# ScalarE takes a third batch of the neighbour rows in the second graph-attention layer

## The chip, the cores and the metric

The kernel runs on one core of a Trainium2 chip. TensorE (PE) multiplies, VectorE (DVE) works element by element and reduces, ScalarE (ACT) applies functions with a scale, GpSimd (POOL) issues the indirect DMAs and SyncE (SP) the plain ones. The metric is the device time of one execution in microseconds. Times are medians of several executions; a difference under 0.3% (10.3 us) is about what a measurement of this kernel cannot tell from no change.

## The reference

There are four layers on x (8 batches, 2048 nodes, 128 features) and one adjacency matrix with 0.8% ones. Layers 0 and 1 are transformer layers with masked attention. Layers 2 and 3 are graph-attention (GAT) layers:

```python
h = x @ W                                   # x: (8, 2048, 128)
e = (h @ a_src)[:, :, None] + (h @ a_dst)[:, None, :]
e = where(e >= 0, e, 0.2 * e);  e = where(adj == 0, -inf, e)
out = einsum('bij,bjd->bid', softmax(e), h)
y = out + x
x = layernorm(y) * ln_gamma + ln_beta
```

## The kernel before, in words

The nodes are sorted by their number of neighbours and cut into 16 tiles of 128 nodes, one node to a partition. `CAPS` (line 38) gives how many neighbour columns each tile has, from 30 down to 11, 277 in all. For every layer a table in device memory has one row per node. In layers 2 and 3 a row has 1040 floats: the projected features of the 8 batches (8 x 128) and two exponentials of the source score for each batch. The neighbours of a tile are fetched column by column: `gather` (line 319, the DMA on line 320) is one indirect DMA by GpSimd that brings the row of the k-th neighbour of each of 128 nodes.

In the GAT layers up to four columns form a chunk. A chunk lands in one of six buffers (`KVB`, line 31), and `gat_chunk` (line 736) is a generator with four steps:

1. DVE finishes the two exponentials (L753), takes their maximum, which is the softmax weight, for all batches into PSUM (`pair`, L754), and once more into a small SBUF tile `ws` for the batches that ACT will scale (L759).
2. DVE multiplies the feature rows of the first `nv` batches with their weights in one instruction (L765). ACT multiplies those of the last `SCALED` batches, one instruction for each column and batch (L770), reading its weight from `ws`.
3. DVE adds the second half of the columns to the first half, all batches (L774).
4. PE adds the remaining columns into the accumulator in PSUM with an identity matrix (L780).

The order is written out by hand: each engine executes its instructions in the order in which the Python code records them. The loop in `layers` (line 1169) records for chunk c steps 1 and 2 and then steps 3 and 4 of the chunk before it, so L774 of chunk c-1 stands behind L765 of chunk c on DVE. Between the steps `slot` (line 1120) advances the tails of finished tiles by one step each and calls `fetch` (line 1096), which records the gathers of chunks up to four ahead. A buffer's new gathers therefore stand in GpSimd's queue behind whatever was recorded earlier, and wait for the PE instructions that last read the buffer.

When the last chunk of a tile is through, `outputs` (L657) divides by the sum of weights and `gat_tail` (line 786) follows: PE adds the residual (L801, L805, L810), ACT squares with an accumulated sum (L817), GpSimd takes the power -1/2 (`rs`, L844), ACT scales by it (L825). In layer 2 the result is then transposed and projected (L329, L832, L535, L549 to L555) and `put_rows` (L502) scatters it into the next layer's table. In layer 3 the layer norm's gain and offset follow on DVE (L858, L860) and GpSimd scatters the tile to the output (L862). In layer 3 the tile `rows`, of which there is one, holds the squares and then the result, so L817 of the next tile waits until L862 has landed.

Layer 3 starts before layer 2 is through: the first two tiles have their neighbour lists sorted by when the neighbour's row is written, and `ORDER` (line 43) puts seven chunks of them first; `fetch` (L1106) holds their gathers until enough tiles of the table are written. While that lasts, `hurry` (line 1115) advances the tails more often.

Of the kernel before, what the change touches and what calls it, by code (L numbers as in the profile page):

```python
# [8 lines left out]
F32 = mybir.dt.float32  # L9
# [8 lines left out]
P = 128  # L18
# [10 lines left out]
NB = 8  # L29
CHUNK = 4 * NB * (D + 2)  # L30
KVB = 6
SCALED = 2

# [47 lines left out]
def sparse_path(ctx: ExitStack, tc: tile.TileContext, ins: dict, out: bass.AP, flag: bass.AP):  # L83
# [10 lines left out]
    nc = tc.nc  # L94
    const = ctx.enter_context(tc.tile_pool(name="const", bufs=1))
    work = ctx.enter_context(tc.tile_pool(name="work", bufs=2))
    small = ctx.enter_context(tc.tile_pool(name="small", bufs=2))
# [5 lines left out]
    def misc():  # L103
        return pm.tile([P, 512], F32, tag="m", name="m")
# [36 lines left out]
    bufs = [const.tile([P, CHUNK], F32, name=f"kv{i}") for i in range(KVB)]  # L141
# [300 lines left out]
    def folded_sums(w, box):  # L442

        columns = w.shape[-1]
        ps = misc()[:, :columns]
        for i in range(FOLD):
            nc.tensor.matmul(ps, merge, w[:, i, :], start=i == 0, stop=i == FOLD - 1)
        box["folded"] = small.tile([P, columns], F32, tag="folded", name="folded", bufs=1)
        nc.scalar.copy(box["folded"], ps)
# [286 lines left out]
    def gat_chunk(l, c):  # L736
        box, t, k, ns = c["box"], c["t"], c["k"], c["ns"]
        mine = own[:, t, :]
        if c["folded"]:
            pf = misc()[:, :NB]  # L740
            nc.tensor.matmul(pf, spread, mine, start=True, stop=True)
            mine = small.tile([P, NB], F32, tag="mine", name="mine", bufs=1)
            nc.scalar.copy(mine, pf)
            yield
        if k == 0:
            box["acc"] = pacc.tile([P, NB // 4, 512], F32, tag="acc", name="acc")
            at, n = (0 if t % 2 == 0 else 512 - NB * CAPS[t]), CAPS[t]
            box["w"] = pair[:, at : at + NB * n].rearrange("p (s b) -> p s b", b=NB)
        acc, w = box["acc"], box["w"]
        hs = c["buf"]  # L750
        wc = w[:, k : k + ns, :]
        wa, wb = hs[:, :, NB * D : NB * (D + 1)], hs[:, :, NB * (D + 1) :]
        nc.vector.tensor_mul(wb, wb, mine[:, None, :].to_broadcast([P, ns, NB]))  # L753
        nc.vector.tensor_max(wc, wa, wb)  # L754
        if c["folded"]:
            box["wf"] = small.tile([P, FOLD, NB], F32, tag="wf", name="wf", bufs=1)
            nc.vector.tensor_max(box["wf"], wa, wb)
        ws = small.tile([P, 4, SCALED], F32, tag="ws", name="ws", bufs=3)
        nc.vector.tensor_max(  # L759
            ws[:, :ns, :], wa[:, :, NB - SCALED :], wb[:, :, NB - SCALED :]  # L760
        )
        yield
        hv = hs[:, :, : NB * D].rearrange("p s (b c) -> p s b c", b=NB)
        nv = NB - SCALED
        nc.vector.tensor_mul(  # L765
            hv[:, :, :nv, :], hv[:, :, :nv, :], wc[:, :, :nv, None].to_broadcast([P, ns, nv, D])
        )
        for i in range(ns):
            for b in range(nv, NB):
                nc.scalar.mul(hv[:, i, b, :], hv[:, i, b, :], ws[:, i, b - nv : b - nv + 1])  # L770
        yield
        left = -(-ns // 2)
        if ns > 1:
            nc.vector.tensor_add(hv[:, : ns - left], hv[:, : ns - left], hv[:, left:ns])  # L774
        yield
        if c["folded"]:
            folded_sums(box["wf"], box)
        for i in range(left):
            for j in range(NB // 4):
                nc.tensor.matmul(  # L780
                    acc[:, j, :], merge if c["folded"] else ident, hv[:, i, 4 * j : 4 * j + 4, :],
                    start=k + i == 0, stop=c["last"] and i == left - 1,
                )
        yield
# [296 lines left out]
    for l in range(4):  # L1081
        per = 2 if l < 2 else 4
        for t, k, ns, folded in pieces(l, per):
            c = dict(l=l, t=t, k=k, ns=ns, folded=folded, box=blocks[l][t])
            c["last"] = not folded and k + ns == (CAPS[t] if t > 0 else BASE)
            c["run"] = (attention_chunk if l < 2 else gat_chunk)(l, c)
            every.append(c)
# [660 lines left out]
```

## Time and profile before

| | |
|---|---|
| device time, median of 3 runs | 3423.61 us (3417.87 to 3426.96) |
| the profiled execution | 3428.05 us, span 3426.3 us |
| layer 2 alone, about | 2220 to 2840 us of the span |
| layer 3, its first chunks among the last tails of layer 2 | from about 2813 us of the span |
| layer 3 alone | about 2884 us to the end |
| busy in 2884 to 3365 us (481 us) | DVE 405.50, POOL 374.36, PE 338.82, ACT 209.82 us; DMA engines 88% |

In a list of instructions a line has the start and the duration in us, the engine, the source line, the operation, the tiles written and read, and a count of equal instructions that followed one another; in brackets stands how long the engine had been idle before it and what released it. In the table of groups, a line has the count, the busy time, the mean duration of one instruction in ns (a third number is idle time before the group) and the releasers.

### The profile page before, as it was taken

To read this page: it belongs to the slowest core of one execution; us is meant where nothing else is said; L and a number is where in the kernel's file an instruction comes from. 1 tells how busy PE (TensorE), PEld (TensorE's weight loads), DVE (VectorE), ACT (ScalarE), POOL (GpSimd) and SP (SyncE) were. 2 spreads that over 40 slices of the span, in tenths; PEclk is the share of its full clock that TensorE was granted. 3 is DMA by queue.
4 is the path that set the end of the run, shared out by engine and by line. 5 is a ranking of instruction groups with operands and counts; after the bars stand their busy time and mean duration, and the time that the engine had idled before them with its cause. 6 is when DMAs were issued, how large, how long until landed. Compare 5 with 4: busy or idle time off the path is not lost.

```text
span 3426.3 us, 34767 instructions
## 1 busy us (share of the span) xinstructions
PE 2761.3 (81%) x10618; PEld 1595.4 (47%) x10618; DVE 3051.6 (89%) x2807; ACT 1425.1 (42%) x4972; POOL 2229.1 (65%) x1453
## 2 busy tenths in 40 slices
PE   5657888788899996888889899976888986767775
PEld 4523445455555652545455555553444543333332
DVE  8799999999999989999999999947867866889885
ACT  4712333334344441333334344453545654445444
POOL 0065888687667654566677666637767865788773
PEclk9888999999999999999999999998988998888887
DMA  8697778888878777677888888658988986899873
GB/s 326 201 355 275 284 283 303 307 303 301 312 290 296 277 287 280 238 309 284 335 298 292 315 297 295 241 171 307 326 290 311 352 326 214 291 313 334 304 275 118
DMA packets 200625, 986.52 MB, mean 288 GB/s; under 512 B 31918, under 2 KB 33712, under 8 KB 128436
## 3 DMA queue, kind: packets, MB, share of 16 engines
q0 software_dynamic: 175024, 890.45, 72.2%
q1 hardware_dynamic: 20502, 75.52, 5.9%
q10 hardware_dynamic: 4904, 18.24, 1.7%
q8 instruction: 87, 1.43, 0.2%
q14 instruction: 108, 0.88, 0.1%
HBM read 937.16 MB, written 91.55 MB: 300 GB/s over the span
## 4 chain that ended last, share of the span: by engine, by line
DVE 36%; PE 23%; issue 19%; DMA 11%; POOL 4%; ACT 4%; POOLq 0%; ACTq 0%; DVEq 0%; another core or an unknown queue 0%
DVE kv L614 13%; DVE kv L628 13%; PE acc L780 7%; PE acc L638 5%; DMA kv<-table,lists 4%; POOL kv L320 3%; DVE sc L617 3%; DMA kv<-table,sorted_lists 2%; DVE kv L774 2%; PE m L329 2%; DVE kv L765 2%; DMA table<-rows,perm 1%; DMA xs<-in_x_nodes_dram,perm 1%; PE m L720 1%; DVE w L459 1%
## 5 line engine op out<-in xcount | busy, mean ns | idle before, releaser
L320 POOL DMA_INDIRECT kv<-table,lists x955 | 1463.0, 1532 | 381.6 <-issue 203.6
L638 PE MATMUL acc<-kv,ident 128*128 128x512 f32 x2200 | 1109.0, 634 | 221.8 <-DVE kv L628 221.3
L780 PE MATMUL acc<-kv,ident 128*128 128x512 f32 x1184 | 622.2, 679 | 190.9 <-DVE kv L774 157.7
L638 PEld LDWEIGHTS acc<-kv,ident 128*128 128x128 f32 x2200 | 413.1, 201 | 652.7 <-issue 365.9
L617 DVE TENSOR_REDUCE sc<-kv 128x128 f32<-128x2048 f32 (+1 forms) x284 | 634.0, 2233 | 9.2
L628 DVE TENSOR_TENSOR kv<-kv,w 128x2048 f32<-128x2048 f32 (+1 forms) x284 | 631.5, 2223 | 8.6 <-ACT w L623 7.9
L614 DVE TENSOR_TENSOR kv<-kv,q 128x2048 f32<-128x2048 f32 (+1 forms) x282 | 629.2, 2231 | 10.7 <-DMA kv<-table,sorted_lists 5.7
L780 PEld LDWEIGHTS acc<-kv,ident 128*128 128x128 f32 x1184 | 248.9, 220 | 514.4 <-issue 294.8
L765 DVE TENSOR_TENSOR kv<-kv,pair 128x3072 f32<-128x3072 f32 (+1 forms) x150 | 466.2, 3108 | 1.0
L484 POOL TENSOR_TENSOR rs<-ss,half 128x4 f32<-128x4 f32 x128 | 222.8, 1741 | 313.9 <-ACT n L479 313.0
L774 DVE TENSOR_TENSOR kv<-kv 128x2048 f32<-128x2048 f32 (+1 forms) x150 | 296.1, 1974 | 145.9 <-ACT kv L770 137.0
L770 ACT ACTIVATE kv<-kv,ws 128x128 f32<-128x128 f32 x1108 | 339.0, 406 | 175.2 <-DVE ws L759 108.9
L479 ACT ACTIVATE n<-m,eps 128x128 f32<-128x128 f32 x512 | 181.0, 366 | 423.6 <-PE m L720 212.5
L623 ACT ACTIVATE w<-sc,lmask 128x64 f32<-128x64 f32 x554 | 165.1, 352 | 443.8 <-DVE sc L617 425.5
L320 POOL DMA_INDIRECT kv<-table,sorted_lists x153 | 203.5, 1330 | 114.8 <-PE acc L638 45.9
L488 ACT ACTIVATE n<-m,rs 128x128 f32<-128x128 f32 x512 | 146.0, 370 | 124.4 <-POOL rs L484 124.2
L502 POOL DMA_INDIRECT table<-rows,perm x57 | 102.5, 1798 | 129.1 <-ACT rows L553 33.2
L329 PE MATMUL m<-ident,n 128*128 128x128 f32 x640 | 105.2, 287 | 67.3 <-ACT n L825 47.4
L720 PE MATMUL m<-w_L_w,hT 128*128 128x128 f32 x1024 | 156.6, 275 | 1.7 <-ACT hT L704 1.7
L329 PEld LDWEIGHTS m<-ident,n 128*128 128x128 f32 x640 | 82.4, 147 | 132.6 <-ACT n L825 57.6
L720 PEld LDWEIGHTS m<-w_L_w,hT 128*128 128x128 f32 x1024 | 135.2, 192 | 1.9 <-ACT hT L704 1.9
L699 PE MATMUL m<-n1T,w_L_gnn_W 128*128 128x512 f32 x256 | 131.6, 597 | 0.8 <-ACT n1T L694 0.4
(242 smaller groups left out, 3476.4 us busy)
## 6 DMA issues: line engine op xcount, KB each, us to landing
kept<-xT SPq DMA_DIRECT2D x48, 512.0 KB
xT<-kept SPq DMA_DIRECT2D x48, 512.0 KB
kv<-in_adj_dram SPq DMA_DIRECT2D x16, 1024.0 KB
table<-kv ACTq DMA_DIRECT2D x16, 1024.0 KB
kv<-table,lists POOLq DMA_INDIRECT x955
kv<-in_x_nodes_dram SPq DMA_DIRECT2D x16, 512.0 KB
kv<-table,sorted_lists POOLq DMA_INDIRECT x153
found<-cand POOLq DMA_DIRECT2D x16, 64.0 KB
```

What stands on the lines that cost most here:

```text
L320: nc.gpsimd.indirect_dma_start(out=dst, out_offset=None, in_=tables[l][:, :], in_offset=bass.IndirectOffsetOnAxis(ap=index, axis=0), bound ...
L329: nc.tensor.transpose(pt[:, j * P : (j + 1) * P], src[:, j, :], ident)
L484: nc.gpsimd.tensor_tensor(rs, ss, half[:, :4], op=ALU.pow)
L614: nc.vector.tensor_mul(kk, kk, q[:, None].to_broadcast([P, ns, NB, D]))
L617: nc.vector.tensor_reduce(sc[:, :ns].rearrange("p s (b h) -> p (s b) h", h=NH), kk.rearrange("p s b (h j) -> p (s b) h j", h=NH), axis=AX. ...
L628: nc.vector.tensor_mul(vv, vv, w[:, k : k + ns, :].rearrange("p s (b h) -> p (s b) h", h=NH)[:, :, None, :] .to_broadcast([P, ns * NB, HD, ...
L638: nc.tensor.matmul(acc[:, j, :], merge if c["folded"] else ident, kv[:, i, 4 * j : 4 * j + 4, D:], start=k + i == 0, stop=c["last"] and i ...
L720: nc.tensor.matmul(y[:, j, :], hT[:, f, j, :], wt["2"][:, f, :], start=False, stop=f == 1, skip_group_check=True,)
L765: nc.vector.tensor_mul(hv[:, :, :nv, :], hv[:, :, :nv, :], wc[:, :, :nv, None].to_broadcast([P, ns, nv, D]))
L770: nc.scalar.mul(hv[:, i, b, :], hv[:, i, b, :], ws[:, i, b - nv : b - nv + 1])
L774: nc.vector.tensor_add(hv[:, : ns - left], hv[:, : ns - left], hv[:, left:ns])
L780: nc.tensor.matmul(acc[:, j, :], merge if c["folded"] else ident, hv[:, i, 4 * j : 4 * j + 4, :], start=k + i == 0, stop=c["last"] and i = ...
```

## The change

`SCALED`, the number of batches that ACT scales, becomes a tuple by layer: two in layer 2 as before, three in layer 3. So in layer 3, L765 covers five batches in place of six and L770 has three instructions for each column in place of two. The tile `ws` is made three wide for both layers, so that in layer 2 only two of three elements in each row of it are written.

```diff
-SCALED = 2
+SCALED = (0, 0, 2, 3)
...
-        ws = small.tile([P, 4, SCALED], F32, tag="ws", name="ws", bufs=3)
-        nc.vector.tensor_max(
-            ws[:, :ns, :], wa[:, :, NB - SCALED :], wb[:, :, NB - SCALED :]
-        )
+        nv = NB - SCALED[l]
+        ws = small.tile([P, 4, max(SCALED)], F32, tag="ws", name="ws", bufs=3)
+        nc.vector.tensor_max(ws[:, :ns, : SCALED[l]], wa[:, :, nv:], wb[:, :, nv:])
         yield
         hv = hs[:, :, : NB * D].rearrange("p s (b c) -> p s b c", b=NB)
-        nv = NB - SCALED
         nc.vector.tensor_mul(
             hv[:, :, :nv, :], hv[:, :, :nv, :], wc[:, :, :nv, None].to_broadcast([P, ns, nv, D])
         )
         for i in range(ns):
             for b in range(nv, NB):
                 nc.scalar.mul(hv[:, i, b, :], hv[:, i, b, :], ws[:, i, b - nv : b - nv + 1])
```

The order of the instructions on every engine is the same as before. The ACT queue has 277 more instructions; no DMA, no matmul and no wait of another kind is added. The new file is two lines shorter, so lines behind L761 have numbers that are two lower in it.

## The prediction

> **What bounds the kernel now.** The change touches layer 3 alone, so I read the table of groups for the sizes and then lists of instructions of that layer. In the table of groups DVE's multiplication L765 and ACT's L770 are the two sides of the edit, and L774 and the gathers L320 stand between them and the next chunk:
>
> ```profile
> L320 POOL DMA_INDIRECT kv<-table,lists x955 | 1463.0, 1532 | 381.6 <-issue 203.6
> ...
> L765 DVE TENSOR_TENSOR kv<-kv,pair 128x3072 f32<-128x3072 f32 (+1 forms) x150 | 466.2, 3108 | 1.0
> ...
> L774 DVE TENSOR_TENSOR kv<-kv 128x2048 f32<-128x2048 f32 (+1 forms) x150 | 296.1, 1974 | 145.9 <-ACT kv L770 137.0
> L770 ACT ACTIVATE kv<-kv,ws 128x128 f32<-128x128 f32 x1108 | 339.0, 406 | 175.2 <-DVE ws L759 108.9
> ```
>
> L774 waits 137.0 us for ACT over both layers, though ACT is only 42% busy: ACT's queue stands still behind something else. Which engine keeps the time shows in the list of instructions of a tile in the middle of layer 3:
>
> ```profile
> 3000.74 3.35 DVE L765 TENSOR_TENSOR kv<-kv,pair 128x3072 f32<-128x3072 f32 x1
> ...
> 3003.07 1.00 POOL L320 DMA_INDIRECT kv<-table,lists  x1 [0.31 <-PE acc L780]
> 3004.01 2.29 DVE L774 TENSOR_TENSOR kv<-kv 128x2048 f32<-128x2048 f32 x1
> 3004.38 2.79 POOL L320 DMA_INDIRECT kv<-table,lists  x1 [0.30 <-issue]
> 3007.47 0.99 POOL L320 DMA_INDIRECT kv<-table,lists  x1 [0.30 <-issue]
> ...
> 3022.69 1.67 POOL L844 TENSOR_TENSOR rs<-ss,half 128x8 f32<-128x8 f32 x1
> ...
> 3024.40 2.17 ACT L825 ACTIVATE rows<-m,rs 128x128 f32<-128x128 f32 x8 [12.85 <-POOL rs L844]
> ...
> 3026.60 1.22 DVE L858 TENSOR_TENSOR rows<-rows,last_g 128x1024 f32<-128x1024 f32 x1 [3.57 <-ACT rows L825]
> ```
>
> POOL goes from issue to issue with a fixed gap of 0.30 us: it waits for nobody. Its own work is long because a gather beside L774 takes 2.79 us in place of 0.99; beside L765 it is not stretched. The power L844 stands in POOL's queue behind those gathers, L825 waits 12.85 us for it on ACT, and L858 on DVE waits 3.57 us for L825. From 2884 to 3365 us of the span POOL is busy 374.4 of 481 us, and its idle time is 81.3 us of gaps before DMA issues (262 of them, nearly all at 0.30 us) and 28.2 us before L844. So DVE, 84% busy there (405.5 us), is not the bound: POOL is.
>
> From about 3220 us the tiles are short and POOL does wait, in one place:
>
> ```profile
> 3250.84 0.37 ACT L817 ACTIVATE rows<-m,eps 128x128 f32<-128x128 f32 x1 [11.26 <-DMA out_dram<-rows,perm]
> ...
> 3253.59 1.88 ACT L770 ACTIVATE kv<-kv,ws 128x128 f32<-128x128 f32 x6
> 3253.88 1.67 POOL L844 TENSOR_TENSOR rs<-ss,half 128x8 f32<-128x8 f32 x1 [3.96 <-ACT rows L817]
> ...
> 3255.50 1.23 DVE L774 TENSOR_TENSOR kv<-kv 128x1024 f32<-128x1024 f32 x1 [3.28 <-ACT kv L770]
> ...
> 3261.48 0.99 POOL L320 DMA_INDIRECT kv<-table,lists  x1 [0.30 <-PE acc L780]
> ```
>
> It is a loop: the output scatter lands, ACT squares (L817, 2.75 us), POOL takes the power, issues the next 13 to 16 gathers and then the next scatter (issued at 3243.80 and 3274.32). L770 stands behind L817 in the queue but not in the loop. DVE's L860, which the scatter needs, starts at 3232.14 and is done at 3233.4, 10.4 us before POOL gets to it.
>
> [...] L774 has both inputs in SBUF and stretches the gather (2.79 us), L765 takes its weights from PSUM and does not (1.00 us). So the edit shortens just the DVE instruction that never held POOL up. [...]
>
> **The change part by part.** *L765 gets shorter.* 3072 elements take 3.353 us, 2304 take 2.552, 1536 take 1.754: 1.042 ns for an element. 2560 elements are then 2.82 us, a saving of 0.53 us for a chunk of four columns, 0.40 for three. Over 277 columns of 128 elements it is 277 x 128 x 1.042 ns = 36.9 us of DVE time. From 2884 to 3365 us I price that at nothing: where POOL keeps the time, DVE reaches L858 sooner and waits longer there (3.57 us becomes about 5.5). Were DVE the bound, it would be a gain (first rival).
>
> *L770 gets longer.* Eight take 2.45 us, sixteen 4.79: 0.2925 us for each further one. Layer 3 gets 277 more, 81.0 us of ACT. A group of eight becomes twelve (+1.17 us), of six nine (+0.88). Where it counts depends on what is behind it.
>
> (a) In the middle of layer 3 (2884 to 3220 us) nothing waits: L774 of a chunk stands behind L765 of the next, and the sixteen L770 behind L825 (4.79 us, now about 7.1) are needed in two halves. From 3026.41 the first twelve are done at 3029.9, and DVE gets to its L774 at about 3031.6; the second twelve at 3033.4, needed about 3037. Cost 0. L817 behind an L770 group had 1.9 us or more in hand on every tile looked at (it waits for the scatter or for PE).
>
> (b) In the short tiles (3222 to 3343 us, five with gathers behind L844) L774 waits for the group behind L817 and starts 0.88 or 1.17 us later. Queued behind it on DVE are the next chunk's steps and L858, with 10 us in hand; behind it on PE is L780, which frees a buffer. In the tile shown PE's sixth matmul ends at 3261.14 and the gather starts at 3261.48, so there is 0.04 us in hand beyond the fixed gap. Three of the five tiles show such a gather (3231.44, 3261.48, 3321.68), two do not. Against it, a later L774 lets the first gather behind L844 (1.92 us, would be 1.0) slip through, which gives about 0.4 back. I take 3 x 0.9 - 3 x 0.4 = +1.5 us; ends -2 (only the slipping) and +5 (five tiles in full).
>
> (c) Seven chunks of layer 3 run among the last tails of layer 2, where ACT is on the path to the table:
>
> ```profile
> 2841.19 2.44 ACT L770 ACTIVATE kv<-kv,ws 128x128 f32<-128x128 f32 x8
> ...
> 2843.54 0.57 ACT L549 COPY rows<-m 128x512 f32<-128x512 f32 x1
> ...
> 2844.51 2.33 POOL L502 DMA_INDIRECT table<-rows,perm  x1 [5.44 <-ACT rows L553]
> ...
> 2875.46 2.44 ACT L770 ACTIVATE kv<-kv,ws 128x128 f32<-128x128 f32 x8
> ...
> 2878.80 2.36 POOL L502 DMA_INDIRECT table<-rows,perm  x1 [13.30 <-ACT score L555]
> ```
>
> L549 to L555 write the rows and stand directly behind L770; POOL waits for them with the scatter, and the gathers wait for its landing (2844.51 to 2852.17). Both groups count in full, since PE's input of L549 is ready before the longer L770 ends (2842.4 against 2844.7): +1.17 each, +2.3 us. The groups at 2832.14, 2850.39 and 2866.54 are hidden: L535 on PE stands behind L780 of an earlier chunk until 2838.0 and 2872.4, and the squares wait for POOL until 2863.82. Those at 2878.49 and 2884.88 are behind the last scatter's inputs. Ends: +1.2 (one group) and +5.9 (all five).
>
> (d) At the end POOL has no gathers left and L862 waits 9.88 us for DVE. The chain L817, L770 (3374.25, eight), L774, L858, L765, L860, L862 gets +1.17 for L770 and -0.40 for L765: +0.8 us.
>
> (e) L759 writes 12 elements in place of 8, and in layer 2 with a stride; 24-element and 32-element neighbours of it (L754) differ by 12 ns, so 74 times nothing.
>
> Sum: 2.3 + 0.8 + 1.5 = +4.6 us. The profiled execution, 3426.3 us of span and 1.75 around it, would be 3432.7; on the median, 3423.6 + 4.6 = **3428 us**.
>
> **The rivals.** *DVE is the bound after all.* For it: it is the busiest engine, 84 to 90% from 2900 to 3200 us, and has the largest share of the chain that ended last (36%). 43 L765 lie in that stretch; at 0.5 us each 21.5 us go, 3405 with (b), (c), (d). Against it: POOL's gaps at 0.30 us, and L858, which waits for POOL by way of L825. If POOL lost less to L774 when DVE ran ahead, this would come true in part.
>
> *ACT becomes the gate of every tile, and it is slower.* One mechanism: L774 behind L817 is late by 1.17 us, PE frees the buffer late, POOL's gather waits. It decides once PE's release is the later one, 0.04 us away in the tile shown. On all 13 tiles with L844 in 2884 to 3365 us it would cost 15.2, with (c) and (d) 18.3: 3442. Against it: in the long tiles POOL is chunks behind the releases, and L825 comes behind L844 and not behind ACT's load.
>
> *The edit does nothing visible*: (b) and (c) fall to their low ends, 3423.6 - 2 + 1.2 + 0.8, 3424; in the same class as the forecast.
>
> **How the numbers follow.** POOL keeps the time, with the last case: 0.62, own range 3416 to 3434. DVE bound in part or whole: 0.12, 3400 to 3413. ACT the gate: 0.26, 3434 to 3448. The first counts as the same (10.3 us is 0.3%, about what a measurement can tell from no change). Leaving out half of the gain's and a third of the loss's cases, the range is 3409 to 3443.
>
> **What would show it.** L765 at 2.82 us for four columns; ACT's busy time up by about 81 us and DVE's down by 37; L858's wait for L825 up by about 2 us a tile; POOL still at gaps of 0.30 us in 2890 to 3220; the first gather of `lists` in layer 3 about 2 us later. It is wrong if the stretch from there to the last gather changes by more than 5 us: shorter says DVE was the bound, longer, with POOL waiting for L780, says ACT is the gate.

## The result: 0.3% faster, and the profile after

The changed kernel takes 3410.31 us (median of 13 runs, 3402.48 to 3415.62) against 3419.58 us of the kernel before in as many runs beside it: a ratio of 0.997, interval 0.996 to 0.9981. The forecast of 3428 us was for +4.6 us; the kernel became 9.3 us shorter. That is just under the 10.3 us that a few runs cannot tell from no change, but with 13 runs of each the interval ends below 1, and two further chips, below, agree. The profiled execution took 3415.62 us with a span of 3413.8 us, against 3428.05 and 3426.3 before.

The two sides of the edit came out as priced. DVE's busy time fell from 3051.6 to 3015.0 us (-36.6; priced at -36.9), ACT's rose from 1425.1 to 1505.9 us (+80.8; priced at +81). From the table of groups of the changed kernel (numbers of lines behind L761 are two lower; the columns are as in the prediction):

```profile
L320 POOL DMA_INDIRECT kv<-table,lists x955 | 1461.0, 1530 | 373.0 <-issue 195.8
...
L763 DVE TENSOR_TENSOR kv<-kv,pair 128x3072 f32<-128x3072 f32 (+3 forms) x150 | 429.2, 2861 | 0.9
...
L772 DVE TENSOR_TENSOR kv<-kv 128x2048 f32<-128x2048 f32 (+1 forms) x150 | 296.3, 1975 | 160.9 <-ACT kv L768 156.2
L768 ACT ACTIVATE kv<-kv,ws 128x128 f32<-128x128 f32 x1385 | 420.0, 407 | 125.0 <-DVE ws L760 81.0
```

What the whole page hides is in the stretch that the prediction worried about, from the first gather of `lists` behind the last table scatter to the end of the last gather. These are POOL's groups in that stretch, of the kernel before (2884.3 to 3364.6 us) and of the changed one (2878.2 to 3351.5 us):

```profile
L320 POOL DMA_INDIRECT kv<-table,lists x226 | 307.3, 1360 | 70.3 <-issue 46.6 <-PE acc L780 7.2 <-DMA kv<-table,lists 6.4
...
L844 POOL TENSOR_TENSOR rs<-ss,half 128x8 f32<-128x8 f32 x13 | 22.2, 1709 | 28.2 <-ACT rows L817 28.1
```

```profile
L320 POOL DMA_INDIRECT kv<-table,lists x226 | 294.5, 1303 | 71.0 <-issue 46.6 <-PE acc L778 6.9 <-DMA kv<-table,lists 6.1
...
L842 POOL TENSOR_TENSOR rs<-ss,half 128x8 f32<-128x8 f32 x13 | 24.6, 1895 | 28.7 <-ACT rows L815 28.6
```

The same 226 gathers, the same gaps ahead of them (70.3 and 71.0 us), the same wait for ACT's squares (28.1 and 28.6 us): POOL is as saturated as before. But its gathers have become shorter, 1303 ns in place of 1360. The time came out of POOL's own instructions, which the edit doesn't touch.

So I take this stretch apart as a sum that can be read from every profile: POOL's work if nothing held it up (each DMA issue at 1.00 us, each L844 at 1.67 us, a fixed gap behind each), which is 360 us in all of them, plus *stretch* (what the issues took above 1.00 us and L844 above 1.67), plus POOL's wait ahead of L844, plus rare other gaps of 0 to 2.2 us (5.6 in one run below). Before: 359.8 + 92.3 + 28.1 = 480.2 us. After: 359.8 + 84.0 + 28.6 + 0.7 = 473.1 us.

Where an issue is stretched is seen in the list of instructions at one tile's end. The kernel before, behind the L858 at 3026.60 that the prediction shows (columns: start, duration, engine and line; only POOL and the large DVE instructions are copied):

```profile
3027.22 1.47 POOL L320 DMA_INDIRECT kv<-table,lists  x1 [0.30 <-issue]
3027.74 3.35 DVE L765 TENSOR_TENSOR kv<-kv,pair 128x3072 f32<-128x3072 f32 x1
3029.00 1.00 POOL L320 DMA_INDIRECT kv<-table,lists  x1 [0.31 <-issue]
3030.30 0.99 POOL L320 DMA_INDIRECT kv<-table,lists  x1 [0.30 <-issue]
3031.01 1.22 DVE L860 TENSOR_TENSOR rows<-rows,last_b 128x1024 f32<-128x1024 f32 x1
3031.60 1.50 POOL L320 DMA_INDIRECT kv<-table,lists  x1 [0.30 <-DMA kv<-table,lists]
```

The same place in the changed kernel:

```profile
3016.53 1.23 DVE L856 TENSOR_TENSOR rows<-rows,last_g 128x1024 f32<-128x1024 f32 x1 [2.56 <-ACT rows L823]
3017.15 1.48 POOL L320 DMA_INDIRECT kv<-table,lists  x1 [0.30 <-issue]
3017.67 2.81 DVE L763 TENSOR_TENSOR kv<-kv,pair 128x2560 f32<-128x2560 f32 x1
3018.93 1.00 POOL L320 DMA_INDIRECT kv<-table,lists  x1 [0.31 <-DMA kv<-table,lists]
3020.24 1.00 POOL L320 DMA_INDIRECT kv<-table,lists  x1 [0.30 <-issue]
3020.40 1.22 DVE L858 TENSOR_TENSOR rows<-rows,last_b 128x1024 f32<-128x1024 f32 x1
3021.54 1.00 POOL L320 DMA_INDIRECT kv<-table,lists  x1 [0.31 <-issue]
```

Three things are to be seen. A gather that begins while a DVE instruction with both inputs in SBUF runs ends 0.87 us after that instruction: before, L858 ends at 3027.82 and the gather at 3028.69, L860 at 3032.23 and the gather at 3033.10; after, 3017.76 and 3018.63. Of POOL's DMA issues in this stretch before, 83 began under L774, L858 or L860 and took over 1.02 us; each ended 0.85 to 0.94 us after the DVE instruction. A gather that began before the DVE instruction isn't stretched: 3020.24, 0.16 us ahead of L858 of the changed kernel. And the end of the held gather sets POOL's beat anew: the next gathers begin about 1.2, 2.5 and 3.8 us after the DVE instruction's end, in both kernels. Whether L860 (`last_b`) meets one depends on how long the multiplication between the two instructions is. At 3.35 us, L860 runs from 3.2 to 4.4 us on this clock, and the beat at 3.8 begins under it; at 2.81 us it runs from 2.6 to 3.9 and the beat comes 0.08 us ahead of its end, too late to matter: 0.08 and 0.87 us are less than the 1.00 us that the gather takes anyway. Over the 13 tiles, L860 stretched a gather 13 times before (7.5 us in all) and twice after (1.2 us).

### The profile page after: what moved, and what is told of

Its sections match the earlier page's. It is cut to its first block, busy times and chain, and to the rows that moved or that the text cites. A ratio compares the mean times of both kernels' runs of the same rounds, so it can differ in the third digit from the quotient of the medians.

```text
span 3413.8 us, 35044 instructions
## 1 busy us (share of the span) xinstructions
PE 2750.0 (81%) x10618; PEld 1587.3 (46%) x10618; DVE 3015.0 (88%) x2807; ACT 1505.9 (44%) x5249; POOL 2221.7 (65%) x1453
## 4 chain that ended last, share of the span: by engine, by line
DVE 36%; PE 20%; issue 20%; DMA 11%; POOL 5%; ACT 4%; POOLq 0%; DVEq 0%; another core or an unknown queue 0%; ACTq 0%
DVE kv L628 13%; DVE kv L614 13%; PE acc L778 6%; PE acc L638 5%; DMA kv<-table,lists 4%; POOL kv L320 3%; DMA kv<-table,sorted_lists 3%; DVE sc L617 2%; DVE kv L772 2%; DVE kv L763 2%; PE m L720 1%; DMA out_dram<-rows,perm 1%; PE m L329 1%; DMA xs<-in_x_nodes_dram,perm 1%; DVE w L459 1%
## 5 line engine op out<-in xcount | busy, mean ns | idle before, releaser
L778 PE MATMUL acc<-kv,ident 128*128 128x512 f32 x1184 | 616.3, 673 | 194.8 <-DVE kv L772 165.3
L778 PEld LDWEIGHTS acc<-kv,ident 128*128 128x128 f32 x1184 | 246.3, 217 | 514.6 <-issue 293.0
L768 ACT ACTIVATE kv<-kv,ws 128x128 f32<-128x128 f32 x1385 | 420.0, 407 | 125.0 <-DVE ws L760 81.0
L763 DVE TENSOR_TENSOR kv<-kv,pair 128x3072 f32<-128x3072 f32 (+3 forms) x150 | 429.2, 2861 | 0.9
L502 POOL DMA_INDIRECT table<-rows,perm x57 | 95.6, 1678 | 130.5 <-ACT rows L553 35.0
L329 PEld LDWEIGHTS m<-ident,n 128*128 128x128 f32 x640 | 82.1, 147 | 129.4 <-ACT n L823 55.1
```

What stands on the lines that cost most here:

```text
L329: nc.tensor.transpose(pt[:, j * P : (j + 1) * P], src[:, j, :], ident)
L763: nc.vector.tensor_mul(hv[:, :, :nv, :], hv[:, :, :nv, :], wc[:, :, :nv, None].to_broadcast([P, ns, nv, D]))
L778: nc.tensor.matmul(acc[:, j, :], merge if c["folded"] else ident, hv[:, i, 4 * j : 4 * j + 4, :], start=k + i == 0, stop=c["last"] and i = ...
```

## The experiments

The theory that I formed from this: POOL is the bound, and the edit changes *when* DVE's two-input instructions fall on POOL's beat (the phase between the two), and so its stretch. Its rivals: DVE is the bound and 36.9 us less of its work is the gain; ACT's longer L770, which delays L774, is what gains; the layout of `ws`, or chance in layer 2, moves the start of layer 3.

All profiles in one table. Lengths are in us, from the first gather of `lists` behind the last table scatter to the end of the last gather; "long" is the part up to the start of the ninth of the 13 L844, about the long tiles, "short" the rest, five tiles in which POOL does wait for ACT. Each length and stretch is one profile's, each ratio is to the kernel before on the same chip.

| kernel | ratio (95%) | length = long + short | stretch, long + short | wait ahead of L844 |
|---|---|---|---|---|
| before | | 480.2 = 338.6 + 141.6 | 68.6 + 23.8 | 28.1 |
| the same file (e16) | 1.0001 (0.999 to 1.0013) | 484.1 = 339.2 + 144.9 | 68.8 + 23.7 | 31.7 |
| only `ws` wider (e1) | 1.0003 (0.999 to 1.0016) | 480.7 = 339.2 + 141.5 | 67.8 + 23.8 | 29.2 |
| **the change** | 0.997 (0.996 to 0.9981) | 473.1 = 332.9 + 140.2 | 61.3 + 22.7 | 28.6 |
| the change (e14) | 0.9955 (0.9938 to 0.9972) | 469.6 = 329.4 + 140.2 | 57.3 + 22.7 | 29.0 |
| the change (e17) | 0.9969 (0.9959 to 0.9978) | 470.0 = 329.0 + 141.0 | 56.8 + 22.7 | 29.9 |
| DVE's part alone (e2) | 0.9977 (0.9964 to 0.999) | 476.6 = 331.3 + 145.3 | 60.3 + 24.5 | 32.0 |
| ACT's part alone (e3) | 0.9964 (0.9949 to 0.9979) | 467.6 = 335.4 + 132.2 | 64.2 + 15.7 | 27.1 |
| first chunks undone (e4) | 0.9973 (0.9961 to 0.9985) | 467.5 = 327.7 + 139.8 | 55.1 + 22.7 | 29.2 |
| four batches on DVE (e5) | 1.0002 (0.9992 to 1.0011) | 477.8 = 328.0 + 149.8 | 56.6 + 29.6 | 31.8 |
| DVE longer, two inputs in SBUF (e7) | 0.9973 (0.996 to 0.9986) | 477.9 = 337.5 + 140.4 | 65.3 + 28.2 | 24.1 |
| DVE longer, one input in SBUF (e8) | 0.9946 (0.9925 to 0.9966) | 460.0 = 329.3 + 130.7 | 56.0 + 16.3 | 22.3 |
| L774 of one column (e9) | 0.9869 (0.9849 to 0.9889) | 436.0 = 307.5 + 128.5 | 29.0 + 12.7 | 33.1 |
| the change and that (e10) | 0.9842 (0.9826 to 0.9858) | 420.2 = 292.5 + 127.7 | 19.7 + 11.5 | 28.6 |
| the same (e18) | 0.9852 (0.9827 to 0.9877) | 423.8 = 294.4 + 129.4 | 21.0 + 11.6 | 30.6 |
| L774 of one column in both layers (e12) | 0.9845 (0.9829 to 0.9862) | 432.6 = 303.2 + 129.4 | 30.5 + 12.7 | 29.7 |
| the change and that (e15) | 0.9951 (0.9935 to 0.9967) | 445.4 = 318.7 + 126.8 | 21.3 + 11.5 | 50.6 |
| the same (e19) | 0.9817 (0.9792 to 0.9842) | 422.4 = 294.7 + 127.7 | 20.2 + 12.5 | 29.4 |

### The two halves of the edit, the layout and the boundary

**Only the tile is wider.** `SCALED` stays at two for both layers, `ws` is three wide.

```diff
-SCALED = (0, 0, 2, 3)
+SCALED = (0, 0, 2, 2)
...
-        ws = small.tile([P, 4, max(SCALED)], F32, tag="ws", name="ws", bufs=3)
+        ws = small.tile([P, 4, 3], F32, tag="ws", name="ws", bufs=3)
```

> Before, with the tile ws three wide but two batches on ScalarE in both layers: only the layout of ws changes. If the part of the gain that the profile shows before layer 3 begins (7.2 of 12.5 us, one execution each) is chance, the ratio is 1.000 within 0.001. If it comes from the layout, about 0.998. The stretching of GpSimd's issues in layer 3 stays near the 92 us of before.

1.0003, and every part of the length as before (stretch 91.6 against 92.3). The layout does nothing. Yet this profile entered layer 3 earlier than both others: the third-last power of layer 2 stands at 2790.5 us, at 2802.2 before and 2795.0 in the changed kernel. Up to there its code differs from before in that one stride only, so some us ahead of layer 3 come from the chip or by chance, and 7.2 of the 12.5 us between the spans of the first two profiles lie there.

**DVE's part alone.** L765 multiplies five batches, L770 two, so the sixth stays unscaled.

```diff
+MINE = (0, 0, 6, 5)
...
+        md = MINE[l]
         nc.vector.tensor_mul(
-            hv[:, :, :nv, :], hv[:, :, :nv, :], wc[:, :, :nv, None].to_broadcast([P, ns, nv, D])
+            hv[:, :, :md, :], hv[:, :, :md, :], wc[:, :, :md, None].to_broadcast([P, ns, md, D])
         )
```

> DVE multiplies five batches in layer 3, ScalarE two as before; the sixth batch is left unscaled (left out). Shorter L765 alone. Phase theory (GpSimd keeps the time; the length of L765 decides which DVE instruction with two SBUF inputs catches a gather): the gain of the change plus what ScalarE cost at the boundary and the end (about 2 us): ratio 0.996 to 0.9975, the last multiplication of the tail (last_b) stretching no more than 2 or 3 of 13 issues. DVE-bound theory: clearly more than the change, ratio 0.993 or less.

0.9977, with the long part 7 to 8 us shorter and L860 stretching a gather on 2 of 13 tiles (1.2 us), as in the changed kernel. In the short part it is the other way: 145.3 us against 141.5 to 144.9 in the three profiles with L765 as before.

**ACT's part alone.** DVE as before; ACT does one scaling more per column into a tile that nobody reads.

```diff
+            if l == 3:
+                junk = small.tile([P, D], F32, tag="junk", name="junk", bufs=1)
+                nc.scalar.mul(junk, hv[:, i, NB - 1, :], ws[:, i, 1:2])
```

> DVE keeps six batches, ScalarE scales two and once more one of them into a scratch tile for each column in layer 3: the longer L770 alone. Phase theory: stretching as before (about 92 us), the costs at the boundary and the end of 2 to 3 us, ratio 1.0005 to 1.002. ScalarE as gate of every tile: about 18 us, ratio 1.005. If it is faster than before, the gain comes from ScalarE's delay of L774 and not from DVE's saving.

This went against my theory as I had put it: 0.9964, and a stretch of 79.9 us where I had written that it would stay. L860 does stretch a gather on all 13 tiles again (7.1 us), but the gain is elsewhere: a smaller part in the long tiles (335.4 us in place of 338.6 to 339.2), the larger in the short ones, 132.2 us, with a stretch of 15.7 in place of 23.8. There POOL does wait for ACT's squares, so that L844 and the gathers behind it stand at a fixed distance from L774 behind the same squares. The list of instructions of such a tile, first of the kernel before:

```profile
3255.74 1.92 POOL L320 DMA_INDIRECT kv<-table,lists  x1 [0.20 <-issue]
3257.78 1.23 DVE L858 TENSOR_TENSOR rows<-rows,last_g 128x1024 f32<-128x1024 f32 x1 [0.66 <-ACT rows L825]
3257.97 1.91 POOL L320 DMA_INDIRECT kv<-table,lists  x1 [0.30 <-issue]
```

Then the changed kernel:

```profile
3242.26 1.06 POOL L320 DMA_INDIRECT kv<-table,lists  x1 [0.19 <-issue]
3242.88 1.22 DVE L772 TENSOR_TENSOR kv<-kv 128x1024 f32<-128x1024 f32 x1 [3.24 <-ACT kv L768]
3243.63 1.34 POOL L320 DMA_INDIRECT kv<-table,lists  x1 [0.30 <-issue]
3244.94 1.23 DVE L856 TENSOR_TENSOR rows<-rows,last_g 128x1024 f32<-128x1024 f32 x1 [0.43 <-ACT rows L823]
3245.28 1.75 POOL L320 DMA_INDIRECT kv<-table,lists  x1 [0.30 <-issue]
```

And ACT's part alone, where L859 is the instruction with `last_g`:

```profile
3248.49 1.06 POOL L320 DMA_INDIRECT kv<-table,lists  x1 [0.19 <-issue]
3249.12 1.23 DVE L775 TENSOR_TENSOR kv<-kv 128x1024 f32<-128x1024 f32 x1 [3.17 <-ACT kv L768]
3249.86 1.35 POOL L320 DMA_INDIRECT kv<-table,lists  x1 [0.31 <-issue]
3251.52 0.99 POOL L320 DMA_INDIRECT kv<-table,lists  x1 [0.30 <-issue]
3251.62 1.23 DVE L859 TENSOR_TENSOR rows<-rows,last_g 128x1024 f32<-128x1024 f32 x1 [0.87 <-ACT rows L826]
```

Before, two gathers are held fully (1.92 and 1.91 us), as L774 began 0.24 us ahead of the first. With a later L774 the first slips through in both (1.06 us) and the second is held for a short while (1.34 and 1.35 us). The third is then a matter of 0.1 us: in the changed kernel it begins 0.34 us after the `last_g` instruction and takes 1.75 us, in e3 0.10 us ahead of it and takes 0.99. The spare instruction writes another tile, and with it a column costs ACT 1.02 us, not the 0.88 us of the change; that is enough to change sides. So e3 is not the change's second half to the letter, and its 10 us are not a share of the change's gain. I had written ahead of it that a faster e3 would put the gain down to ACT's delay of L774; against that stands that e3 gains mostly in the short tiles, and the change, like e2, in the long ones. In the short tiles ACT's delay does play a part in the change too, as these lists show.

**The first chunks undone.** The change, but the chunks of layer 3 among the last tails of layer 2 keep two batches on ACT.

```diff
+        sc = 2 if l == 3 and t < 2 and not c["folded"] and k + ns <= (16, 12)[t] else SCALED[l]
```

> The change, but the seven chunks of layer 3 that run among the last tails of layer 2 keep two batches on ScalarE. My step (c) said 2.3 us there: ratio to before 0.0007 below the change's 0.997, the time from the last layer-2 power but two to the first gather of lists 1.2 to 2.3 us shorter than in the change's profile. If (c) is nothing, the same as the change.

0.9973 with the change at 0.997, 0.9955 and 0.9969: undoing these chunks brings nothing that can be told from the change. From the third-last power of layer 2 to the last table scatter it was 76.6 us before, 76.1 in e1, 77.8 in the changed kernel, 77.4 here, 74.9 in e2 and 79.5 in e3. The spread of these figures is as large as the +2.3 us that I had priced, and the 1.2 to 2.3 us that I had expected to get back came to 0.4. Only the last step shows ACT's load, from the last power of layer 2 to the last scatter: with L774 as before it is 14.6 to 15.5 us in the eight profiles with two scalings a column there (15.0 before, 15.5 here), and 15.7 to 17.0 in the four with three (16.5 in the changed kernel).

### Is DVE the bound?

If it is, still less DVE work must be still faster, and more of it slower. Three kernels: four batches on DVE (two stay unscaled), and two that add an instruction of one batch behind L765, one with both inputs in SBUF (a maximum of the batch with itself, which changes no value), one that takes its weights from PSUM (the first batch is scaled twice).

```diff
-MINE = (0, 0, 6, 5)
+MINE = (0, 0, 6, 4)
```

> As the run with five batches on DVE and two on ScalarE, but DVE multiplies four (two batches are left unscaled, left out). L765 of four columns is 2.29 us. DVE-bound theory: a further 9 to 18 us gone, ratio 0.994 or less. Phase theory: [...] last_b [...] stretches 10 or more of 13 issues, by 0.7 us each, 8 to 10 us in all in place of 1.2; layer 3's gathers take 470 to 485 us and equal 360 us plus stretch plus the wait of the power.

```diff
+        if l == 3:
+            nc.vector.tensor_max(hv[:, :, 0, :], hv[:, :, 0, :], hv[:, :, 0, :])
```

> Before, with one more DVE instruction for each chunk of layer 3 directly behind L765: the maximum of one batch with itself in place, two SBUF inputs, 512 elements, about 0.69 us. Phase theory: each holds GpSimd up for some 0.6 us more: gathers of layer 3 take 505 to 525 us in place of 480, ratio 1.007 to 1.013. DVE-bound theory: 67 x 0.62 = 42 us, ratio 1.012[...].

```diff
+        if l == 3:
+            nc.vector.tensor_mul(
+                hv[:, :, 0, :], hv[:, :, 0, :], wc[:, :, 0, None].to_broadcast([P, ns, D])
+            )
```

> Before, with the same DVE time added in the same place, but one of the two inputs in PSUM: one batch is multiplied by its weight a second time (so the result is not the layer's). Phase theory: at most 10 us, from other phases or from DVE coming near to its own limit, ratio 0.998 to 1.003. DVE-bound theory: ratio 1.012.

DVE is not the bound. With four batches on DVE, one batch in each of the 277 columns less than in e2, the time is that of before (1.0002). The list of instructions of its middle tile (L321 is the gather here):

```profile
3012.75 2.28 DVE L765 TENSOR_TENSOR kv<-kv,pair 128x2048 f32<-128x2048 f32 x1
3014.01 0.99 POOL L321 DMA_INDIRECT kv<-table,lists  x1 [0.30 <-DMA kv<-table,lists]
3014.95 1.22 DVE L860 TENSOR_TENSOR rows<-rows,last_b 128x1024 f32<-128x1024 f32 x1
3015.31 1.73 POOL L321 DMA_INDIRECT kv<-table,lists  x1 [0.30 <-issue]
```

L860 comes another 0.53 us earlier and now meets the beat before, at 2.5 us: 13 of 13 tiles again, 8.4 us, as I had expected (10 or more tiles, 8 to 10 us). That is not the whole of it. The long part stayed as short as with the change (328.0 us), because the long L774 held POOL for less time (58.7 us over both parts, 68.6 before); it is the short part that grew, to 149.8 us with a stretch of 29.6. I had foreseen L860, but neither of these.

The other direction is the clearer one. In e8 a chunk of four columns costs DVE 0.69 us more, and the kernel is 19 us *faster* (3402.37 against 3421.79). POOL's and DVE's groups of e8 between its first and last gather (2876.4 to 3336.6 us; L778 is the addition L774, L769 the added instruction):

```profile
L320 POOL DMA_INDIRECT kv<-table,lists x226 | 285.5, 1263 | 75.7 <-issue 47.6 <-PE acc L784 12.3 <-DVE kv L765 3.8
...
L778 DVE TENSOR_TENSOR kv<-kv 128x2048 f32<-128x2048 f32 (+1 forms) x66 | 128.8, 1952 | 3.1 <-ACT kv L774 3.1
L769 DVE TENSOR_TENSOR kv<-kv,pair 128x512 f32<-128x512 f32 (+1 forms) x66 | 42.4, 642 | 2.3
```

DVE is busy 442.0 of 460.2 us there, against 404.8 of 480.3 before: its waits were filled with work, and the stretch fell by 20 us, the length by as much. I had expected 0.998 to 1.003 for it, so here too the size of a shift in phase was not foreseen. In e7 the expectation failed as well: 0.69 us more per chunk in which gathers can be held were to cost 25 us and more, but the kernel ran 0.3% faster and the stretch came out at 93.5 us. The added instruction held POOL for 5.4 us and the short L774 for 15.3 in place of 7.5, while `last_b` held it for 0.6 in place of 7.5 and the long L774 for 63.4 in place of 68.6. The instruction that holds didn't add its length here; it moved where the others fell. The pair does show which instruction holds: in e8, 38 of POOL's DMA issues began under the added instruction, with one input in PSUM, and none took longer than 1.05 us; in e7, 25 of the 31 that began under it ended 0.9 us after it, as under L774 (five began within 0.03 us of its start and passed, one fell to the L774 behind it). Why e7 and e8 come to *just* these sums I haven't derived.

### Take the largest holder away

L774 adds half of a chunk's columns to the other half, 2.29 us for four columns. This edit lets it add one column only, in layer 3, and PE takes three in place of two (L780).

```diff
-        left = -(-ns // 2)
+        left = -(-ns // 2) if l == 2 else max(ns - 1, 1)
```

> Before, but in layer 3 L774 adds only the last column of a chunk of four to the first, and PE accumulates three columns in place of two: 44 or more instructions with two SBUF inputs go from 2.29 to 1.23 us, and PE gets 8 to 4 = 4 more matmuls of 0.6 to 0.7 us in each such chunk. Phase theory: about 1 us less stretch on each of 44: gathers of layer 3 take 435 to 450 us, ratio 0.989 to 0.992. If PE becomes the bound instead (339 us busy of 481 before, some 110 more), 0.993 to 1.0. DVE-bound theory: 44 x 1.06 = 47 us, ratio 0.987.

Length 436.0 us, stretch 41.7 in place of 92.3, ratio 0.9869: 45 us by the medians, 44 by the length. The ratio is below the 0.989 to 0.992 that I had expected, and is where the theory of a DVE bound had put it (0.987); so it is the stretch, 50.6 us less, together with e5 and e8, that tells the two apart, and not the ratio. POOL's group between first and last gather (2871.9 to 3308.1 us), and two places of the list of instructions:

```profile
L320 POOL DMA_INDIRECT kv<-table,lists x226 | 263.0, 1164 | 73.7 <-issue 46.3 <-PE acc L780 17.5 <-DMA kv<-table,lists 4.0
```

```profile
3004.34 1.22 DVE L774 TENSOR_TENSOR kv<-kv 128x1024 f32<-128x1024 f32 x1
3005.59 1.00 POOL L320 DMA_INDIRECT kv<-table,lists  x1 [0.30 <-DMA kv<-table,lists]
...
3009.27 1.22 DVE L774 TENSOR_TENSOR kv<-kv 128x1024 f32<-128x1024 f32 x1
3009.49 1.86 POOL L320 DMA_INDIRECT kv<-table,lists  x1 [0.30 <-issue]
```

A holder of 1.22 us is shorter than POOL's beat of 1.30 us: it can miss every gather, as the first here, and one that it meets loses 0.9 us here, at most 1.02 us in this profile, and not up to the 2.09 us that a 2.29-us one cost before. PE's 39 us of added work (377.3 us busy in place of 338.1) cost little: POOL's idle time ahead of these gathers rose from 70.3 to 73.7 us.

The same on top of the change; on the kernel before in both layers; and on the change in both layers:

> The change together with the one-column addition L774 in layer 3. Phase theory: the gathers of layer 3 take 360 us plus stretch (25 to 50) plus waits of the power (about 33): 418 to 443 us; the third batch on ScalarE adds no gain of its own in a fixed direction: ratio to before between 0.984 and 0.990. DVE-bound theory: the two gains add up, 0.984 or less.

> Before with the one-column addition L774 in both GAT layers. If GpSimd keeps the time in layer 2 as it does in layer 3, a further 20 to 40 us, ratio 0.976 to 0.982. If PE or the tails bound layer 2 (PE 497 of 620 us busy there), 0.984 to 0.992.

> The change together with the one-column addition L774 in both GAT layers. [...] in layer 3 as with the change and the one-column addition there (gathers 415 to 430 us, stretch 25 to 40), in layer 2 a small gain as in the run with both layers: ratio to before 0.980 to 0.984.

The change and the one-column L774 together give 0.9842, with 31.2 us of stretch left. The same gathers then take 420.2 us with the DMA engines 93% busy, against 88% in 480 us before, so the DMA engines, which I hadn't named as a rival, were not what kept the time either. In both layers, without the change, it is 0.9845, with a length of 432.6 us, close to e9's: layer 2 brings little that can be told, which fits PE (busy 497.2 of the 620 us of layer 2 before) or the tails as its bound. The fourth kernel gave 0.9951, far from 0.980 to 0.984, though its stretch (32.8 us) is as small as e10's. On that chip its layer 2 ended late (last scatter at 2895.7 us) and POOL waited 50.6 us ahead of L842, mostly because ACT's squares waited for PE.

### The same files on one more chip

> The change itself, a second profile. If the smaller stretch in layer 3 belongs to the change and not to one execution: gathers of layer 3 take 471 to 475 us, stretch 82 to 86, last_b stretches at most 3 of 13 issues, ratio 0.996 to 0.998.

> Before itself, a second profile, on one chip with the change. [...] gathers of layer 3 in 479 to 482 us, stretch 91 to 93, wait of the power 28 to 29, last_b stretches 13 of 13 issues; ratio 1.000 within 0.0015.

> The change itself, a third profile, on the chip of the second profile of before. Gathers of layer 3 in 468 to 474 us, stretch 80 to 84, last_b stretches 2 of 13; what it is shorter than before from the last power but two of layer 2 to the end is 5 to 9 us. If the ratio is again 0.997 or less while this is only 5 us, a part of the gain lies before layer 3 and is not explained[...].

> The change with the one-column addition in layer 3, on another chip than before. If what made the combination with both layers slow (0.9951) is the chip or PE's clock on it, this is slow too here, 0.990 to 0.995, with the power waiting 45 us or more in layer 3. If it is the addition in layer 2, this stays at 0.983 to 0.986.

> The change with the one-column addition in both GAT layers, once more, beside its partner with the addition in layer 3 alone. If the addition in layer 2 costs (PE becomes the bound there), 0.993 to 0.997 again, the last scatter into the table 20 us or more later than in the partner; if the chip did it, within 0.003 of the partner.

The change as it is gave 0.9955 and 0.9969 on two further chips, with stretches of 80.0 and 79.5 us (e14's length, stretch and ratio and e17's stretch a little below what I had written), and L860 stretching a gather on 2 of 13 tiles in each; the kernel before gave 1.0001 against itself, with 13 of 13 and a stretch of 92.5 us (its length, 484.1 us, and its wait ahead of L844, 31.7 us, were longer than expected). From the third-last power of layer 2 to the end, e17 is 11.5 us shorter than e16, where I had expected 5 to 9; the first pair of profiles has 5.2, with 9.3 by the medians. One profile of each is that loose a measure. e18 repeats e10. The kernel that gave 0.9951 in e15 is the fastest of all here, 0.9817 (0.9792 to 0.9842), 3330.29 us with e18 at 3340.79: 0.0035 below its partner, a little outside the 0.003 that I had written for the case that the chip was the reason; the addition in layer 2 gains here, if anything. The groups of ACT's squares, of e15 and then of e19, over the whole span:

```profile
L815 ACT ACTIVATE rows<-m,eps 128x128 f32<-128x128 f32 x128 | 45.0, 373 | 136.4 <-PE acc L778 78.3 <-DMA out_dram<-rows,perm 49.7 <-issue 5.8
```

```profile
L815 ACT ACTIVATE rows<-m,eps 128x128 f32<-128x128 f32 x128 | 45.0, 372 | 105.7 <-DMA out_dram<-rows,perm 73.6 <-PE m L808 16.7 <-PE acc L778 15.5
```

The squares waited 78.3 us for PE on one chip and 15.5 us on the other. What made PE late on the first stays open; I would ship e10's version, which gave nearly the same on two chips: 1.5% less than the kernel before and 1.2% less than the change.

## Why the prediction was wrong

The time lies inside the range, the sign is wrong. That it lies inside is luck: the range reached below the forecast for the case of a DVE bound, which e5 and e8 refute. By the steps of the prediction:

- **POOL keeps the time, and DVE doesn't.** Right. The gaps at 0.30 us are as before, and e5 and e8 refute the rival in both directions. But the test that I set, "shorter says DVE was the bound", was wrong: the stretch from first to last gather shrank by 7.1 us for a reason that the list did not have. (The sum under that rival is off as well: 3423.6 - 21.5 + 4.6 is 3406.7, not 3405.)
- **L765 shorter, priced at nothing.** This is the step that failed. It took POOL's busy time in this layer as given, so that DVE's gain could only turn into waiting. It did (L774's idle time ahead of it rose from 34.0 to 48.2 us there, that of the exponentials L753 from 7.0 to 15.0, L858's by 2.2 in all and not by 2 us a tile), but POOL's time is partly made by DVE: 92 of 480 us are POOL's instructions held by DVE's two-input ones, and L765 is part of what sets when these start. Over three profiles each (before, e16 and e1, whose layout did nothing; the change, e14 and e17), the long part went from 339.0 to 330.4 us, -8.6, and e2, with this half of the edit alone, has -7.7. e3, ACT's half alone, has -3.6, so the halves don't add up to the whole. I had read from one tile that L774 holds POOL (a gather of 2.79 us) and L765 doesn't (1.00 us), and drew from it that L765's length can't matter to POOL; it sets the moment of the next holder. The remark under the first rival, that POOL might lose less to L774, is what came true in part, without DVE being the bound.
- **Which holders.** POOL's stretch by what held it, mean of the same three profiles each: L860 7.4 to 1.2 us, the 2.29-us L774 68.7 to 63.8, L858 8.1 to 6.4, the 1.22-us L774 7.2 to 9.0; -11.0 together. Of L860 alone the cause is shown down to the beat. For the long L774 the profiles show where the gain sits: a gather held by it began on average 0.64 us after its start before, and 0.71 to 0.77 us with the change. Why it comes later isn't derived, nor are the two smaller terms.
- **(a) The middle, no cost from ACT.** Nothing against it: a longer wait of L774 for L770, and no more wait of gathers for PE (7.2 and 6.9 us).
- **(b) The short tiles, +1.5 us.** They went from 142.7 to 140.5 us (mean of three each), -2.2: the low end, named as "only the slipping". The late release that I counted three times didn't show.
- **(c) The boundary, +2.3 us.** The two groups do count, by more than was priced. POOL's instructions around the last two table scatters of the changed kernel, from its list of instructions:

```profile
2821.63 1.68 POOL L842 TENSOR_TENSOR rs<-ss,half 128x8 f32<-128x8 f32 x1
2838.36 2.33 POOL L502 DMA_INDIRECT table<-rows,perm  x1 [7.21 <-ACT rows L553]
...
2856.35 1.67 POOL L842 TENSOR_TENSOR rs<-ss,half 128x8 f32<-128x8 f32 x1
2872.80 2.36 POOL L502 DMA_INDIRECT table<-rows,perm  x1 [14.77 <-ACT score L555]
```

  From power to scatter it is 16.7 and 16.5 us; before, with the powers at 2829.42 and 2863.82, 15.1 and 15.0. But from the first scatter to the last power 18.0 us stand against 19.3, and over the last three powers +1.2 us is left (76.6 to 77.8). The groups were the right ones; that the part between them isn't fixed was missed.
- **(d) The end, +0.8 us.** After the last gather 61.7 us before and 62.4 after; over three profiles each 61.4 and 63.2, so +0.7 to +1.8.
- **The sum.** -8.6 - 2.2 + 1.2 + 1.8 = -7.8 us, against -9.3, -14.4 and -8.4 by the medians on three chips. The difference on the second isn't placed; the kernel before has no profile on that chip.

The list of the one tile was read too coarsely as well. It shows which DVE instruction holds a gather, and I didn't look at when. What counted in the lists above is which of the two began first: the gather 0.16 us ahead of L858 in the changed kernel ran in 1.00 us, the one 0.62 us behind the start of L858 of the kernel before took 1.47. That makes the cost a matter of phase, and phase is what an edit moves. Much hangs on it: the gathers of the kernel before took from 0.99 to as much as 3.09 us. Why two inputs in SBUF hold a gather, and one in SBUF with one in PSUM doesn't, no run shows.

## What to carry to other kernels

When an engine is saturated, ask whether its own instructions are at their shortest before taking its time as a constant: compare the durations of equal instructions, and look at what runs beside the long ones. Where DVE instructions with two SBUF inputs hold up GpSimd's DMA issues, shortening the long ones was worth much more here (45 us) than moving other work off DVE, and edits of a few tenths of a us between two such instructions moved gathers in and out of their reach by phase, so that the gains of the parts didn't add up. A second profile of each kernel is then needed before a few us are put down to a cause.

## What was not expected of the hardware

The cost of being held fell on one line. In the twelve profiles that have the 2.29-us L774, 519 of POOL's DMA issues in this stretch were held by one; they took 3.05 us when begun within 0.2 us of its start, 2.65 at 0.4 to 0.6 us, 2.26 at 0.8 to 1.0 and 1.90 at 1.2 to 1.4: 3.16 us less the offset, that is the rest of the DVE instruction and 0.87 us, with a standard deviation of 0.01 us. So regular an end ties the long issues to the DVE instruction beside them. With POOL's beat of 1.30 us (an issue of 1.00 and a gap of 0.30) the offset is 0.65 us on average, if phases are even, so a long L774 costs an estimated 3.16 - 0.65 - 1.00 = 1.51 us, and the 45 of them in this stretch 68 us; 68.6 were found before. For the 1.22-us kind, which meets a gather at most once within its length, the same sum gives 2.09 - 0.61 - 1.00 = 0.48 us, a third for about half of the length. And a kernel with 0.69 us more DVE work for each chunk of four columns (e8) ran 0.5% faster (0.9946).
